# Attention and a mixture of experts in one kernel: v's bias folded into the output's bias, v's copies moved to ACT, and v and q of later pairs computed earlier

## The chip, the cores and the metric

The kernel runs on one core of one Trainium2 chip. The time is device microseconds of one execution, the median over several. A core has five engines with a queue each: PE (matrix multiplies; PEld is its loading of the stationary operand), DVE (vector), ACT (activation functions and copies), POOL (here masks, zeroing and indirect DMAs) and SP (here it only issues DMAs). Each engine's instructions appear in the profile in the order of its queue, and one that waits holds up what is behind it.

## The reference

```python
# x: 8 x 512 x 256 (8 batch rows of 512 tokens), 16 heads of 16, window +-64, 8 experts, top 2
xn = _layernorm(x)
qkv = xn @ Wqkv + bqkv;  q, k, v = jnp.split(qkv, 3, axis=-1)
scores = jnp.einsum('bhid,bhjd->bhij', heads(q), heads(k)) * DH ** -0.5
attn = softmax(where(|i - j| <= 64, scores, min))
attn_out = einsum('bhij,bhjd->bhid', attn, heads(v)) -> b n d,  @ Wout + bout
logits = xn @ router_w + router_b;  top 2 of 8, gates = softmax over the two
h = relu(xn @ w1[e] + b1[e]);  y = h @ w2[e] + b2[e]     # w1: 256 x 1024, w2: 1024 x 256
out = x + attn_out + sum over the two experts of gate * y
```

All data are float32. Each token goes to two experts, so 8192 pairs of a token and an expert have to be computed.

## The kernel before

**Stages.** Until about 44 us the kernel normalizes: for each half u of a batch row b (u = 0 to 15) DVE computes statistics (`stats`, `variances`, `inverse`), ACT the root (`root`, a Sqrt) and the normalized rows (`norm`, line 356), PE turns them (`xt`, line 93), and DVE or ACT takes the turned rows out of PSUM (`keep`, lines 378 and 380). PE computes the router's logits for a row (`lg`), ACT copies them (`keep_logits`, line 401, tile `early`), PE turns them (`lt`), DVE adds the bias (`add_bias`, line 410) and picks the two experts (`choose`, lines 449 to 462, in generator steps called by `pick`, for rows 0 to 3, then 4 and 5, then 6 and 7). The loop over u at lines 1096 to 1134 writes out the order of all this.

Then comes the routing (`route`, line 481; about 44 to 65 us). A scan over all chosen pairs (line 485) and three matmuls (`ranks`) give each pair its slot; slots are sorted by expert into 71 tiles of 128. To turn "slot of each token" into "token of each slot" (`inv`), eight chunks of eight columns each build one-hot tiles: DVE makes `pl` (every second chunk) and two planes of `tl` (lines 550 and 556), ACT the third (line 555, an Identity with a scale), and PE adds eight matmuls per chunk into the PSUM tile `inv`. In chunk 1 `experts` finds each tile's expert and issues the loads of the first two tiles' weights on SP (`load_1`, `load_2`; w1 and w2 of 1 MB each). Steps of `share_out` between chunks compute the gates; its last step turns them (`gps`) and writes them to DRAM (`gd`). From `inv`, DVE works out each slot's token (`tok`, lines 573 to 583), and POOL gathers the first three tiles' normalized rows (`xs`, line 685) and gates (`g`).

From then on two streams are interleaved. One is the experts: for each of 69 tiles PE turns the gathered rows (`turn`: `px`, copied by DVE to `xT`), computes the first layer in two halves (`first_layer`: `h`, ACT's Relu to `hT`), and the second (`second_layer`: `y`; DVE scales it to `yo`, and POOL adds it into the output by an indirect DMA). The other is attention, in 16 pairs p (half of the heads of a batch row b = p // 2): `dense(p, 0)` and `dense(p, 1)` compute q and k; `vals(b, t)` computes v of 128 tokens (into `vA`, two buffers, by b % 2); `maxima(p, n)` (through `search`) multiplies q by k (`sc`) and DVE reduces each row (line 903, tiles `jk` and `nm`); `put_maxima` turns the maxima (`nt`) and adds them into q; `weigh` computes the scores the other way (`st`), ACT the exp, POOL cuts the window's edges (lines 957 and 962); `values` multiplies by v (`av`); `put_sums` to `scale` divide by the row sums through DRAM; `project` multiplies by Wout and DVE adds `bo` (line 1065).

**What sets the order.** The order on ACT, DVE, POOL and SP is the program's own (`manual_schedule`), and `pe` chains PE's instructions in program order as well. The streams are interleaved by the loop at line 1183: 69 rounds of two half-rounds each. A half-round does `weigh`, `search`, `values` and the work of `others(p, r)` (dense, vals, project, each with a cost), one step of `divide`, and then as many pieces of the experts' stream (`expert_pieces`, with costs of 9, 16 and 8) as keep the running cost `sofar` in step with `share`. `LAST` pieces are kept for the end. PSUM tiles of tag "m" have three buffers, shared by nearly all matmuls outside the attention's core.

**What the change touches.** `load_others` (line 143) loads `bv`, 128 copies of v's bias; `vals` adds it by DVE (line 873). `qk_bias` (line 266) turns `braw`, the biases of q and k as 4 rows, into `bqk`. `choices` (line 257; nine instructions on DVE) is called at u = 8, and its tile `choice` is read only by `scale_at_once` at the very end. `turn_b1` (line 279; a turn on PE, a copy on ACT and a DMA `b1d` on SP) is called within `route`. Line 1111 says which `keep` goes to ACT. Lines 1142 to 1147 are the order between the front and the loop:

```python
    dense(0, 1)
    route()
    start_experts()
    search(0)
    for t in range(NT):
        vals(0, t)
```

ACT's table of functions is loaded before the first copy (line 169) and again before the first Sqrt (line 329), and before the gates' Exp (line 472).

Of the kernel before, what the change touches and what calls it, by code (L numbers as in the profile page):

```python
# [22 lines left out]
def kernel(  # L23
# [15 lines left out]
    nc = tc.nc  # L39
# [49 lines left out]
    def matmul(*args, **kwargs):  # L89
        return pe(nc.tensor.matmul(*args, **kwargs))  # L90

    def transpose(*args):
        return pe(nc.tensor.transpose(*args))  # L93
# [24 lines left out]
        xt[b] = pair[:, b % 2]  # L118
        nc.sync.dma_start(out=xt[b], in_=x[b].rearrange("(t p) d -> p t d", p=P))

    braw = const.tile([4, A, 32], F32, tag="braw", name="braw")
    for s in range(2):
        nc.scalar.dma_start(
            out=braw[2 * s : 2 * s + 2],
            in_=bqkv[s * D : (s + 1) * D].rearrange("(a i r) -> i a r", i=2, r=32),
        )
# [7 lines left out]
    raw = p_pool.tile([P, KC, 2 * D], F32, tag="p", name="raw")  # L134
    nc.scalar.dma_start(out=raw, in_=wqkv[:, 0 : 2 * D].rearrange("(k p) m -> p k m", p=P))
    wv = const.tile([P, KC, D], F32, tag="wv", name="wv")
    bv = const.tile([P, D], F32, tag="bv", name="bv")
    b1raw = const.tile([E * HC, P], F32, tag="b1raw", name="b1raw")

    wo = const.tile([P, 2, D], F32, tag="wo", name="wo")  # L140
# [2 lines left out]
    def load_others():  # L143
        nc.sync.dma_start(out=b1raw, in_=b1.rearrange("e (c p) -> (e c) p", p=P))
        nc.sync.dma_start(
            out=wv, in_=wqkv[:, 2 * D : 3 * D].rearrange("(k p) m -> p k m", p=P)
        )
        nc.sync.dma_start(out=bv, in_=bqkv[2 * D : 3 * D].partition_broadcast(P))
        for a in range(A):
            nc.sync.dma_start(  # L150
                out=wo[32 * a : 32 * a + 32],
                in_=wout[64 * a : 64 * a + 64].rearrange("(i r) m -> r i m", r=32),
            )
        nc.sync.dma_start(out=bo, in_=bout.partition_broadcast(P))
# [11 lines left out]
    col_i = const.tile([P, P], I32, tag="col_i", name="col_i")  # L166
    nc.gpsimd.iota(col_i, pattern=[[1, P]], base=0, channel_multiplier=0)
    cols = const.tile([P, P, 16], BF16, tag="cols", name="cols")
    nc.scalar.copy(cols, col_i.unsqueeze(2).to_broadcast([P, P, 16]))

    num_i = const.tile([P, 2], I32, tag="num_i", name="num_i")
# [66 lines left out]
    at = const.tile([P, 2], F32, tag="at", name="at")  # L238
    qat = const.tile([P, 2], F32, tag="qat", name="qat")
    hot = const.tile([P, 2], F32, tag="hot", name="hot")  # L240
    bqk = const.tile([P, 2, 2], F32, tag="bqk", name="bqk")

    kb_ = const.tile([P, 2, 2], F32, tag="kb", name="kb")
    qb_ = const.tile([P, 2, 2], F32, tag="qb", name="qb")
# [20 lines left out]

    def qk_bias():
        bps = ps_m.tile([P, 512], F32, tag="m", name="bps")
        transpose(bps[:, 0:4], braw.rearrange("q a r -> q (a r)"), ident[:4, :4])
        nc.scalar.copy(bqk.rearrange("p s i -> p (s i)"), bps[:, 0:4])
        full = [P, 2, 2]  # L270
        for to, s, by in ((kb_, 1, at), (qb_, 0, qat)):
            nc.vector.tensor_mul(
                to, bqk[:, s].unsqueeze(2).to_broadcast(full), by.unsqueeze(1).to_broadcast(full)
            )
        nc.vector.tensor_add(kb_, kb_, hot.unsqueeze(1).to_broadcast(full))

    b1T = const.tile([P, E * HC], F32, tag="b1T", name="b1T")

# [202 lines left out]
    def route():  # L481
# [15 lines left out]
        next(gating)  # L497
        for s in range(2):
            dense(1, s, by_act=True)
        turn_b1()  # L500

        size_i = wk1.tile([P, E], I32, tag="size_i", name="size_i")
        size = wk1.tile([P, E], F32, tag="size", name="size")
# [32 lines left out]
        for c in range(NA * TOPK // C):  # L536
            h = c % 2
            if h == 0:

                pl = o_pool.tile([P, P, C2], BF16, tag="o", name=f"pl_{c}")  # L540
                nc.vector.tensor_tensor(
                    pl, part[:, ts(c // 2, C2)].unsqueeze(1).to_broadcast([P, P, C2]), cols,
                    ALU.is_equal,
                )

            tl = io.tile([P, 8 * D], BF16, tag="xn", name=f"tl_{c}")
            tl = tl[:, 0 : 3 * C * 2 * W].rearrange("p (s n t) -> p s n t", s=3, n=C)
            full = [P, C, W, 2]
            pairs = tl.rearrange("p s n (w i) -> p s n w i", i=2)
            nc.vector.tensor_tensor(  # L550
                pairs[:, 0], twice[:, ts(c, C)].unsqueeze(2).to_broadcast(full),
                colb.rearrange("p (w i) -> p w i", i=2).unsqueeze(1).to_broadcast(full),
                ALU.is_equal,
            )
            nc.scalar.activation(tl[:, 2], tl[:, 0], AF.Identity, scale=num[:, 0:1])
            nc.vector.tensor_mul(
                pairs[:, 1], pairs[:, 0], hn[:, ts(c, C)].unsqueeze(2).to_broadcast(full)
            )
            for n in range(C):
                matmul(  # L560
                    inv.rearrange("p (s t) -> p s t", s=2), pl[:, :, h * C + n],
                    tl[:, 1:3, n, 0:TILES], start=(c + n == 0),
                    stop=(c * C + n == NA * TOPK - 1),
                )
            if c == 1:
                experts(end)
            if c >= 1:
                next(gating, None)
        of_tile, of_part = inv[:, 0:TILES], inv[:, TILES : 2 * TILES]
        row = wk1.tile([P, TILES], F32, tag="row", name="row")  # L570
        row_i = wk1.tile([P, 2, TILES], I32, tag="row_i", name="row_i")
# [14 lines left out]
    def experts(end):  # L586

        past = p_pool.tile([P, TILES, E], F32, tag="p", name="past")
        starts = wk1.tile([P, TILES], F32, tag="starts", name="starts")
        nc.vector.tensor_scalar(starts, col[:, 0:TILES], float(TS), None, ALU.mult)  # L590
        nc.vector.tensor_tensor(
            past, starts.unsqueeze(2).to_broadcast([P, TILES, E]),
            end.unsqueeze(1).to_broadcast([P, TILES, E]), ALU.is_ge,
        )
        ends = wk1.tile([P, TILES], F32, tag="ends", name="ends")
        ef = wk1.tile([P, TILES], F32, tag="ef", name="ef")
        nc.vector.tensor_reduce(ends, past, AX.X, ALU.add)
        nc.vector.tensor_scalar(ef, ends, float(E - 1), None, ALU.min)
        nc.vector.tensor_copy(eid, ef)
        late["ends"] = ends  # L600
        nc.vector.tensor_copy(filled, end[:, E - 1 : E])
        for i in range(2):
            load_1(i)
            load_2(i)

    def put_gates():
        gps = ps_m.tile([P, 512], F32, tag="m", name="gps")
# [254 lines left out]
    def vals(b: int, t: int):  # L862
        pm = ps_m.tile([P, 512], F32, tag="m", name=f"v_{b}_{t}")
        for k in range(KC):
            matmul(
                pm[:, 0:D], xnT[b][:, k, ts(t, P)], wv[:, k, :],
                start=(k == 0), stop=(k == KC - 1),
            )

        to = vA[b % 2][:, t].rearrange("p h j c -> p h (j c)").rearrange(  # L870
            "p h (u d) -> p h u d", d=DH
        )[:, :, 0:4:3, :]
        nc.vector.tensor_add(
            to,
            pm[:, 0:D].rearrange("p (h j d) -> p h j d", j=2, d=DH),
            bv.rearrange("p (h j d) -> p h j d", j=2, d=DH),
        )

    first = [(h, j, ah) for h in range(2) for j in range(2) for ah in range(2)]
    second = [(j, h, ah) for j in range(2) for h in range(2) for ah in range(2)]  # L880
# [215 lines left out]
    for u in range(UNITS + 3):  # L1096
        b = u // 2
        if u < UNITS:
            norm(u, by_dve=False)
        if u in ROOTS:  # L1100
            root(ROOTS[u])
        if u in INVERSES:
            inverse(*INVERSES[u])
        for n in STATS.get(u, ()):
            stats(n)
            if u in VARIANCES and n in (1, VARIANCES[u][1] - 1):
                variances(*VARIANCES[u])
        if u >= 3 and u % 2 == 1 and b - 1 < B:
            keep_logits(b - 1)
        if 0 < u <= UNITS:  # L1110
            keep(u - 1, by_act=u < 7 or u == UNITS)
        if u >= 5 and u % 2 == 1 and b - 2 < B:
            add_bias(b - 2)
        if u == 3:
            load_others()
        if u == 7:
            places()
        if u == 8:
            qk_bias()
            columns()  # L1120
            choices()
            clear()
        if u >= 8 and u % 2 == 0:
            start_result(u // 2 - 4)
        if u >= 2 and u % 2 == 0 and b <= B:
            logits(b - 1)
        if u >= 4 and u % 2 == 0 and b - 2 < B:
            turn_logits(b - 2)
        if u == 11:
            picking.append(choose(0, 4))  # L1130
        if u == 15:
            picking.append(choose(4, 6))
        if u >= 11:
            pick(3)
# [5 lines left out]
    for b in (6, 7):  # L1140
        start_result(b)
    dense(0, 1)
    route()
    start_experts()
    search(0)
    for t in range(NT):
        vals(0, t)

    pieces = expert_pieces()
    ROUNDS = 4 * (PAIRS + 1) + 1

    divide = {1: gather_sums, 2: invert, 3: put_inverses, 4: spread_inverses, 6: scale}
# [3 lines left out]
    def others(p: int, r: int):  # L1159

        out_ = [[], []]
        if p == -1 and r == 0:
            out_[0].append((0, free_rows))
            out_[1].append((2, destinations))
        if 0 <= p < PAIRS - 2 and r < 2:
            out_[r % 2].append((8, lambda: dense(p + 2, r)))

        if 0 <= p < PAIRS - 2 and r in (1, 2):
            out_[r % 2].append((4, lambda: vals(p // 2 + 1, 2 * (p % 2) + r - 1)))

        if 1 < p < PAIRS and p % 2 == 1:
# [89 lines left out]
```

## Time and profile before

| | |
|---|---|
| timed runs | 918.02, 919.34, 919.76 us; median 919.34 |
| profiled execution | 921.26 us |
| its span | 919.6 us |
| busy: PE, DVE, ACT, POOL | 879.8, 405.4, 377.4, 459.0 us |
| mean granted clock of PE | 0.981 |
| HBM read, written | 172.84 MB, 22.18 MB |
| first `xt` on PE | 9.62 us |
| scan of the routing on DVE | 44.04 us |
| first read of the finished `inv` (`row`) | 64.87 us |
| first `xs` gather issued | 66.14 us |
| `vals(0, 0..3)` on PE | 66.56 to 72.9 us |
| first `h` on PE | 77.48 us |
| last `y` on PE begins | 904.84 us |

How to read the lines: in the windows, each engine has its busy time in the stretch and, in brackets, its count of instructions; then the granted clock of PE (1.00 is full speed), the share of the DMA engines' time that packets took, and GB/s. A timeline line is start, duration, engine, line of the kernel, operation, output <- input, shapes, count, and in square brackets how long the engine was idle before it and what ended that. Most PE work is recorded under line 90 or 93, since two helpers issue it; it is told apart by its tiles. A float32 matmul shows as two records.

### The profile page before, as it was taken

To read this page: it belongs to the slowest core of one execution; us is meant where nothing else is said; L and a number is where in the kernel's file an instruction comes from. 1 tells how busy PE (TensorE), PEld (TensorE's weight loads), DVE (VectorE), ACT (ScalarE), POOL (GpSimd) and SP (SyncE) were. 2 spreads that over 40 slices of the span, in tenths; PEclk is the share of its full clock that TensorE was granted. 3 is DMA by queue.
4 is the path that set the end of the run, shared out by engine and by line. 5 is a ranking of instruction groups with operands and counts; after the bars stand their busy time and mean duration, and the time that the engine had idled before them with its cause. 6 is when DMAs were issued, how large, how long until landed. Compare 5 with 4: busy or idle time off the path is not lost. (4 is left out here: it accounts for less than half of the span.)

```text
span 919.6 us, 20413 instructions
## 1 busy us (share of the span) xinstructions
PE 879.8 (96%) x7260; PEld 707.4 (77%) x7260; DVE 405.4 (44%) x1558; ACT 377.4 (41%) x884; POOL 459.0 (50%) x770
## 2 busy tenths in 40 slices
PE   4778999999999999999999999999999999999995
PEld 2457887878878888877878887878787878888884
DVE  6885343444344434453435343534444344330250
ACT  7541234444444344434444443444434343444421
POOL 4013445456465556455546564466456554656512
PEclk9868999999999999999999999999999999999998
DMA  8953876676666767686858676587667775887794
GB/s 287 321 175 99 263 233 208 218 209 222 209 220 206 202 190 236 206 217 181 249 172 231 193 241 193 169 249 226 203 161 230 223 225 174 237 283 229 230 254 69
DMA packets 154044, 196.38 MB, mean 214 GB/s; under 512 B 26174, under 2 KB 131774, under 8 KB 153942
## 3 DMA queue, kind: packets, MB, share of 16 engines
q1 hardware_dynamic: 133554, 172.20, 57.3%
q0 software_dynamic: 19680, 22.33, 13.0%
q8 instruction: 58, 0.95, 0.4%
q10 hardware_dynamic: 708, 0.54, 0.2%
q14 instruction: 44, 0.36, 0.1%
HBM read 172.84 MB, written 22.18 MB: 212 GB/s over the span
## 5 line engine op out<-in xcount | busy, mean ns | idle before, releaser
L752 ACT ACTIVATE hT<-h,b 128x128 f32<-128x128 f32 x552 | 157.3, 368 | 307.7 <-PE h L90 266.9
L90 PEld LDWEIGHTS h<-xT,w 128*128 128x128 f32 x2208 | 261.2, 193 | 26.0 <-issue 16.8
L90 PE MATMUL h<-xT,w 128*128 128x128 f32 x2208 | 270.2, 278 | 3.4 <-DVE xT L736 3.3
L90 PE MATMUL y<-w,hT 128*128 128x256 f32 x1104 | 252.6, 382 | 0.0
L90 PEld LDWEIGHTS y<-w,hT 128*128 128x128 f32 x1104 | 206.4, 190 | 36.4 <-issue 7.9
L768 POOL DMA_INDIRECT out_dram<-yo,dest x69 | 113.1, 1639 | 224.6 <-DVE yo L767 159.1
L903 DVE CUSTOM_DVE_ANT_0 jk<-sc,mask 128x256 bf16<-128x256 f32 (+1 forms) x512 | 169.7, 387 | 99.2 <-PE sc L90 98.3
L957 POOL TENSOR_SCALAR_AFFINE_SELECT p<-p 128x256 f32<-128x256 f32 (+1 forms) x256 | 138.2, 569 | 119.4 <-ACT p L947 109.3
L947 ACT ACTIVATE p<-st 128x896 f32<-128x896 f32 x128 | 117.4, 917 | 184.7 <-PE sc L90 174.9
L962 POOL TENSOR_SCALAR_AFFINE_SELECT p<-p 128x256 f32<-128x256 f32 (+1 forms) x256 | 140.9, 579 | 0.0
L90 PE MATMUL sc<-k,q 32*128 32x192 f32 (+1 forms) x1024 | 132.2, 376 | 0.0
L90 PE MATMUL st<-q,k 32*128 32x192 f32 (+1 forms) x1024 | 131.4, 374 | 0.0
L767 DVE SCALAR_TENSOR_TENSOR yo<-y,g,b2g 128x256 f32<-128x256 f32 x69 | 33.4, 484 | 183.5 <-PE y L90 93.9
L90 PEld LDWEIGHTS st<-q,k 32*128 32x128 f32 x1024 | 83.8, 184 | 26.3 <-issue 20.6
L90 PEld LDWEIGHTS sc<-k,q 32*128 32x128 f32 x1024 | 84.3, 185 | 2.1 <-issue 1.7
L736 DVE COPY xT<-px 128x256 f32<-128x256 f32 x69 | 29.2, 423 | 121.3 <-PE px L93 121.3
L685 POOL DMA_INDIRECT xs<-xd,tok x69 | 70.0, 1015 | 23.9 <-DVE taken L580 9.0
L695 POOL DMA_INDIRECT g<-gd,gate x69 | 65.8, 953 | 22.8 <-issue 20.7
L90 PE MATMUL av<-p,vA 128*32 128x256 f32 (+1 forms) x1024 | 64.7, 359 | 0.4 <-POOL p L962 0.4
L90 PE MATMUL qk<-xnT,wqk 128*128 128x512 f32 x128 | 63.9, 625 | 0.0
L90 PEld LDWEIGHTS av<-p,vA 128*32 128x32 f32 x1024 | 29.9, 109 | 24.2 <-issue 15.5
L903 DVE DVE_READ_ACCUMULATOR2_ANT nm<- 128x1 f32 x512 | 42.5, 83 | 0.0
(176 smaller groups left out, 592.7 us busy)
## 6 DMA issues: line engine op xcount, KB each, us to landing
w<-in_L_ffn_w_dram SPq DMA_DIRECT2D x138, 1024.0 KB
b<-in_L_ffn_b_dram SPq DMA_DIRECT2D x69, 128.0 KB
x<-in_L_attn_x_dram SPq DMA_DIRECT2D x8, 512.0 KB
xd<-xn SPq DMA_DIRECT2D x8, 512.0 KB
out_dram<-x SPq DMA_DIRECT2D x8, 512.0 KB
out_dram<-sum POOLq DMA_DIRECT2D x8, 512.0 KB, 6.1
bc<-d SPq DMA_DIRECT2D x120, 32.0 KB
b<-b1d SPq DMA_DIRECT2D x69, 4.0 KB
```

Of the source, the lines that this page charges most:

```text
L90: return pe(nc.tensor.matmul(*args, **kwargs))
L685: nc.gpsimd.indirect_dma_start(out=tx, out_offset=None, in_=xd, in_offset=bass.IndirectOffsetOnAxis(ap=tok[:, i : i + 1], axis=0),)
L695: nc.gpsimd.indirect_dma_start(out=tg, out_offset=None, in_=gd, in_offset=bass.IndirectOffsetOnAxis(ap=gate[:, i : i + 1], axis=0),)
L736: nc.vector.tensor_copy(s["xT"], px)
L752: nc.scalar.activation(s["hT"][:, c, :], ph[:, n, :], AF.Relu, bias=s["tb"][:, c : c + 1])
L767: nc.vector.scalar_tensor_tensor(yo, py[:, 0:D], s["tg"], b2g, ALU.mult, ALU.add)
L768: nc.gpsimd.indirect_dma_start(out=by_token, out_offset=bass.IndirectOffsetOnAxis(ap=dest[:, i : i + 1], axis=0), in_=yo, in_offset=None, ...
L903: nc.vector.tensor_tensor_reduce(out=junk[:, 0 : hi - lo], in0=sc[c][:, i, 0 : hi - lo], in1=mask[:, off : off + hi - lo], scale=-1.0, sca ...
L947: nc.scalar.activation(w.rearrange("k c i q -> k c (i q)")[:, :, cut], st.rearrange("k c i q -> k c (i q)")[:, :, cut], AF.Exp,)
L957: nc.gpsimd.affine_select(out=one, in_=one, pattern=[[0, 2], [1, P - off]], compare_op=ALU.is_ge, fill=0.0, base=off, channel_multiplier=-1,)
L962: nc.gpsimd.affine_select(out=two, in_=two, pattern=[[0, 2], [-1, end - P]], compare_op=ALU.is_ge, fill=0.0, base=0, channel_multiplier=1,)
```

## The change

- `braw` gets v's bias as a third pair of rows (a third small DMA on ACT's queue), `bqk` a third entry, and the DMA of `bv` goes. `vals` copies v by ACT, without a bias. Since the weights of a softmax sum to 1, v's bias adds bias @ Wout to every token; the new `out_bias` computes that (two broadcast copies on DVE, two matmuls, an add into `bo`).
- Three more `keep` calls (u = 9, 11, 13) go to ACT; `turn_b1` moves to u = 9; `choices` moves from u = 8 into the loop.
- `vals(0, 0)` and `vals(0, 1)` move ahead of `route`, `vals(0, 2)` and `vals(0, 3)` to where `turn_b1` stood in it. `vals(1, 0..3)`, before in the first two pairs of the loop, come after chunks 1, 3, 5 and 6 of `route`. `dense(2, 0)`, before in pair 0, comes after the first `search`.
- The weight loads of the second tile are issued after chunk 4 in place of within `experts`.
- The first tile's `turn` is done before the loop begins, and so ahead of the second unit of maxima.
- A Sqrt of a constant is issued ahead of ACT's first copy; the second table load, ahead of the first root, falls away.

```diff
-    braw = const.tile([4, A, 32], F32, tag="braw", name="braw")
-    for s in range(2):
+    braw = const.tile([6, A, 32], F32, tag="braw", name="braw")
+    for s in range(3):
         nc.scalar.dma_start(
             out=braw[2 * s : 2 * s + 2],
...
-        nc.sync.dma_start(out=bv, in_=bqkv[2 * D : 3 * D].partition_broadcast(P))
...
+    one = const.tile([1, 1], F32, tag="one", name="one")
+    nc.vector.memset(one, 1.0)
+    nc.scalar.activation(one, one, AF.Sqrt)
     nc.scalar.copy(cols, col_i.unsqueeze(2).to_broadcast([P, P, 16]))
...
-        transpose(bps[:, 0:4], braw.rearrange("q a r -> q (a r)"), ident[:4, :4])
-        nc.scalar.copy(bqk.rearrange("p s i -> p (s i)"), bps[:, 0:4])
+        transpose(bps[:, 0:6], braw.rearrange("q a r -> q (a r)"), ident[:6, :6])
+        nc.scalar.copy(bqk.rearrange("p s i -> p (s i)"), bps[:, 0:6])
...
+    def out_bias():
+
+        wide_b = wk.tile([P, 2, P], F32, tag="junk", name="bv")
+        pm = ps_m.tile([P, 512], F32, tag="m", name="bo_")
+        for i in range(2):
+            nc.vector.tensor_copy(wide_b[:, i, :], bqk[:, 2, i : i + 1].to_broadcast([P, P]))
+        for i in range(2):
+            matmul(pm[:, 0:D], wide_b[:, i, :], wo[:, i, :], start=(i == 0), stop=(i == 1))
+        nc.vector.tensor_add(bo, bo, pm[:, 0:D])
...
         for s in range(2):
             dense(1, s, by_act=True)
-        turn_b1()
+        for t in (2, 3):
+            vals(0, t)
...
             if c >= 1:
                 next(gating, None)
+            if c == 4:
+                load_1(1)
+                load_2(1)
+            if c in (1, 3, 5, 6):
+                vals(1, (1, 3, 5, 6).index(c))
...
-        for i in range(2):
-            load_1(i)
-            load_2(i)
+        load_1(0)
+        load_2(0)
...
-        nc.vector.tensor_add(
-            to,
-            pm[:, 0:D].rearrange("p (h j d) -> p h j d", j=2, d=DH),
-            bv.rearrange("p (h j d) -> p h j d", j=2, d=DH),
-        )
+        nc.scalar.copy(to, pm[:, 0:D].rearrange("p (h j d) -> p h j d", j=2, d=DH))
...
-            keep(u - 1, by_act=u < 7 or u == UNITS)
+            keep(u - 1, by_act=u < 7 or u in (9, 11, 13, UNITS))
...
             qk_bias()
             columns()
-            choices()
             clear()
+        if u == 9:
+            turn_b1()
...
     dense(0, 1)
+    for t in (0, 1):
+        vals(0, t)
     route()
     start_experts()
     search(0)
-    for t in range(NT):
-        vals(0, t)
+    dense(2, 0, by_act=True)
...
     pieces = expert_pieces()
+    pieces.pop(0)[1]()
...
+        if p == -1 and r == 1:
+            out_[0].append((4, out_bias))
+        if p == -1 and r == 2:
+            out_[0].append((0, choices))
...
-        if 0 <= p < PAIRS - 2 and r < 2:
+        if 0 <= p < PAIRS - 2 and r < 2 and (p, r) != (0, 0):
             out_[r % 2].append((8, lambda: dense(p + 2, r)))
 
-        if 0 <= p < PAIRS - 2 and r in (1, 2):
+        if 2 <= p < PAIRS - 2 and r in (1, 2):
             out_[r % 2].append((4, lambda: vals(p // 2 + 1, 2 * (p % 2) + r - 1)))
```

More of the change, by code (lines that the diff above doesn't have):

```diff
@@ L136 @@
     wv = const.tile([P, KC, D], F32, tag="wv", name="wv")
-    bv = const.tile([P, D], F32, tag="bv", name="bv")
     b1raw = const.tile([E * HC, P], F32, tag="b1raw", name="b1raw")
@@ L240 @@
     hot = const.tile([P, 2], F32, tag="hot", name="hot")
-    bqk = const.tile([P, 2, 2], F32, tag="bqk", name="bqk")
+    bqk = const.tile([P, 3, 2], F32, tag="bqk", name="bqk")
     kb_ = const.tile([P, 2, 2], F32, tag="kb", name="kb")
```

## The prediction

> **What bounds the kernel now.** I read the page first (busy shares, the 40 slices, the granted clock), then a table by windows, then the timelines of the engines up to 90 us, and the timeline of PE in the middle.
>
> ```profile
> PE 879.8 (96%) x7260; PEld 707.4 (77%) x7260; DVE 405.4 (44%) x1558; ACT 377.4 (41%) x884; POOL 459.0 (50%) x770
> ...
> PE   4778999999999999999999999999999999999995
> ...
> PEclk9868999999999999999999999999999999999998
> ```
>
> PE is full from slice 5 on, and only the first four slices (92 us) have holes. There the clock is also low, and DVE is the busy engine (9.66 us of the ten from 50 to 60). So there are two stages with different prices: the front, where a chain over DVE, ACT and PE decides, and the rest, where each us of PE work is a us of time. The windows say it in numbers (columns: busy us of PE, PEld, DVE, ACT, POOL, then granted clock, DMA share, GB/s):
>
> ```profile
> 51.40:54.80 3.40, 1.34 (x16) 1.27 (x16) 3.23 (x10) 3.37 (x6) 0.00 (x0) 1.00 0.14 10
> 54.80:58.20 3.40, 1.35 (x11) 1.36 (x12) 3.33 (x7) 1.61 (x3) 1.17 (x2) 0.50 0.43 106
> ...
> 71.90:75.30 3.40, 2.30 (x15) 1.35 (x13) 2.28 (x12) 0.00 (x0) 2.72 (x3) 1.00 0.02 2
> 75.30:78.70 3.40, 1.22 (x10) 1.22 (x11) 2.02 (x6) 0.00 (x0) 2.00 (x3) 1.00 0.15 41
> ```
>
> ```profile
> 80.00:905.00 825.00, 824.53 (x6910) 670.95 (x6910) 346.17 (x1363) 335.94 (x804) 435.85 (x717) 1.00 0.71 214
> ```
>
> From 80 to 905 us PE idles 0.5 us of 825 at full clock. The front on PE's timeline:
>
> ```profile
> 52.70 1.34 PE L90 MATMUL inv<-tl,pl 128*128 128x142 bf16 x16 [2.11 <-ACT tl L555]
> 56.85 2.18 PE L90 MATMUL inv<-tl,pl 128*128 128x142 bf16 x16 [2.81 <-ACT tl L555]
> ...
> 60.27 2.05 PE L90 MATMUL inv<-tl,pl 128*128 128x142 bf16 x16 [1.02 <-ACT tl L555]
> 62.78 2.05 PE L90 MATMUL inv<-tl,pl 128*128 128x142 bf16 x16 [0.47 <-DVE tl L550]
> 64.76 1.86 PE L90 MATMUL sc<-k,q 32*128 32x192 f32 x8
> 66.56 6.32 PE L90 MATMUL v<-wv,xnT 128*128 128x256 f32 x16
> ...
> 73.77 0.44 PE L93 MATMUL px<-ident,xs 128*128 128x128 f32 x2
> 77.48 2.71 PE L90 MATMUL h<-xT,w 128*128 128x128 f32 x16 [3.28 <-DVE xT L736]
> ```
>
> Routing ends with the last inv (DVE's row starts at 64.87); xs is fetched at 66.14 and lands 5.9 us later, at about 72.0; v of row 0 fills that time at half clock; and the first h waits 3.28 us because the copy xT stands on DVE behind the second maxima and free_pl:
>
> ```profile
> 26.36 1.48 DVE L261 COPY choice<-hot 32x32 f32<-32x32 f32 x8
> 27.87 0.69 DVE L380 COPY xnT<-xt 128x512 f32<-128x512 f32 x1
> ...
> 75.87 1.22 DVE L634 TENSOR_TENSOR free_pl<-free_at,cols 128x2048 bf16<-128x2048 bf16 x1
> 77.01 0.42 DVE L736 COPY xT<-px 128x256 f32<-128x256 f32 x1
> ```
>
> In the middle, start to start, a dense half (qk) is worth 1.82 us of PE and one vals tile 0.86 us:
>
> ```profile
> 421.65 1.98 PE L90 MATMUL qk<-xnT,wqk 128*128 128x512 f32 x4
> 423.47 1.03 PE L90 MATMUL v<-wv,xnT 128*128 128x256 f32 x4
> 424.33 0.94 PE L90 MATMUL h<-xT,w 128*128 128x128 f32 x7
> ```
>
> **1. Work taken out of the PE-bound stage.** Four vals of row 1 (4 x 0.86) and one dense half of pair 2 (1.82) leave it: -5.26 us. out_bias comes in: four matmuls of 256 columns, 0.86 us. It is called right after the fourth maxima, and its two DVE copies stand behind that unit's four reductions. In the trace this unit's sc ends on PE at about 91.66 and DVE's last read of nm is at 93.01 + 0.08; two broadcast copies of 128x128 follow (col, a cast of that size, takes 0.22), so about 93.45. PE's order is written out by hand, so it stands still for 1.8 us. Bounds: 0.86 (no stall) to 3.5 (stall, and the copies as slow as xT's 0.42 each); I take 2.66, the row's own times. Stage: -2.6 us. choices (1.75 us of DVE: memset 0.27, copies 1.48) lands before an xT copy; DVE idles 2.66 us before those at 95.76 and 105.52, so it costs nothing; without that cover, 1.75. The 24 other vals turn from a DVE add (0.425 each) into an ACT copy. No row has 128x256 from PSUM by ACT; 128x128 takes 0.26 and 128x512 0.58, so 0.37, at most the 0.60 of the norm. That is 9 us on an engine busy 336 of 825, ahead of an exp whose st matmul stands later on PE anyway: nothing.
>
> **2. Front until the scan (44.04 us).** DVE loses choices (1.75) and three keeps (0.6 each, start to start): 3.55 us, in a stretch where it idles under 0.4 us at a time. ACT gets three copies of 0.48 and b1's 0.2; PE gets b1's turn (0.27; b1raw was issued at 16.8, and the DMA share falls to 0.76 at 20 to 22, so it should be there). Bounds: 0 (ACT and PE only pass the wait on) to -3.55. Followed through the queues: keep(9) can start when xt ends at 26.5 and not at 28.70, lg(4) at 28.25 for 28.61, but then ACT's norms (1.04 us for each unit) set the pace; add_bias(5) comes at 35.6 for 37.13, and the 26 small selection steps behind it are serial on DVE. I take -1.4: the scan at 42.6. The early Sqrt removes one table load (1.28) before root(0), less 0.6 for the new activation and DMA issue; but DVE waits for x at 10.86 for 0.59 us already and would wait longer: 0, at best -0.7. The third braw issue moves raw 0.4 us later, and with it POOL's copy into wqk (11.18), which PE first reads at 38.68: 0. SP loses the bv load; b1d moves between two 512 KB writes, which are over long before 55 us: 0.
>
> **3. Routing, 44 to 65 us.** Here the change adds waits. On ACT the four vA copies of row 1 stand in the queue between the tl steps (after chunks 1, 3, 5 and 6), and each waits for a vals that PE does after the inv of the chunk before. So from chunk 4 on ACT and PE take turns: vals, copy, tl, inv. What a turn costs depends on the clock. PE's inv of a chunk takes 0.67 at full clock and 1.02 at half; vals 0.86 and, from 6.32 / 4, 1.58; tl 0.73 on ACT; vA 0.3 to 0.37. Behind the copies stand only tl, gT and the exp; who waits is PE, then row on DVE.
> At half clock, from the shifted DVE times: inv of chunks 2 and 3 55.35 to 57.4, gps 57.8, vals 59.4, vA 59.75, tl 4 60.45, inv 4 and 5 62.5, vals 64.1, vA and tl 6 65.15, inv 66.2, vals 67.8, vA and tl 7 68.85, inv 69.9: row starts at about 69.9, +5.1 against 64.87. At full clock the same turns (inv 0.67, vals 0.86) end at 66.5: +1.6.
> SP issues the second tile's weights behind gd, once chunk 4's step is reached: about 58 to 60, before 58.62 to 60.80; they are first read by the second tile's h, after 80: 0, and gd lands sooner.
> Which clock? The rows show a stretch 39% busy (51.4 to 54.8), one 53% busy (27.5 to 30.9) and one 36% busy (75.3 to 78.7), each followed by 0.50; those 68% and 76% busy (71.9 to 75.3, 48.0 to 51.4) kept 1.00. Once lost, it came back after stretches that were busy throughout (68.5 to 71.9 and 78.7 to 82.1), and not after 70% or 86% (58.2 to 65.0). In the changed kernel 51.4 to 54.8 holds inv of chunk 1 and most of a vals, about 1.8 of 3.4: 53%. I take half clock, by the row at 53%.
> The Trainium skill ("TensorE: Matmul & The Clock Gate", section "HAM oscillation — how this bites in real kernels") puts the rule as no PE idle gaps over about 3.4 us. The longest gap here would be some 2 us, so by the rule the clock stays full and the whole sum would be -8.3; this trace, which lost the clock after 53% busy, speaks against relying on it.
>
> **4. From routing to the first h.** Before: 64.87 to 77.48, 12.6 us. After, at half clock: sc 1.8 us to 71.7; dense of pair 2 (3.64 at half clock, 1.82 at full; PE is full of f32 work, so between) to about 74.5. xs is issued at row + 1.27 = 71.2; the weights are loaded by then (before, they kept the DMA at 1.04 until 71.4, issued from 55.5; now from 54.1), so it lands like the later ones in 2.7 us: 73.9. px 74.5 to 74.8, xT at once (DVE has nothing ahead of it), sc of the second maxima 1.0 to 1.4, h at about 76.2: -1.3. Then the clock: before, h and px from 77.48 to 83.10 took 5.62 us at 0.50 where two halves and a px take 3.96 at full clock. PE is now busy from 68 on, so that returns: -1.7. Front in all: -3.0 (it holds part 2).
>
> **Sum.** -3.0 - 2.6 = -5.6 us against the profiled execution's 921.26 (span 919.6 and 1.7 around it): 915.7. That execution lies 1.9 above the median of 919.34 of the timed ones; there it gives **913.7 us**.
>
> **Rivals.**
> Full clock through routing. For it: vals in every gap. Row at 66.5, h at 73.5 (xs at 70.4, dense at half clock to 72), clock regained: -4.0 - 1.7 - 2.6 = -8.3: 911.0. Chance 0.27.
> The freed PE time is not gained: the tiles then wait for weights, or dense and vals were cover for something. Against: 214 GB/s in the stage, while 20 to 60 us show up to 390. Then only the front's -3.0 stays, or, with the routing turns 2 us longer, only -0.6 or so is left beside the stage's gain: 916 to 918.5. Chance 0.17.
> Slower: ACT's queue. If every vA copy holds tl longer than worked out (PE, at half clock, still in the chunk before; the copy nearer to 0.60; tl late by a buffer), the turns add to row's start one for one. It decides from row at 69.9 + 5.6 = 75.5, and is measurable from 77.3, 1.9 us a turn over the four turns: 922 or so. For it: three of the four inv groups wait for tl already. Against: tl, vA and inv are short. Chance 0.08. The forecast has 0.48.
>
> **How the numbers follow.** 0.2% (1.8 us) is about what a measurement of this kernel can tell from no change. Range: at the low end full clock with 1 us more of part 2's -3.55 (910.0); at the high end half clock with only 1 us of the sum left (918.3). Faster: 0.48 + 0.27 and two thirds of 0.17, 0.86; same 0.06; slower 0.08.
>
> **What would show it.** The scan at 42 to 43; inv in more than four groups with vals between, row at 66 to 71; granted clock 0.50 or not at 55 to 65; xT straight after px, first h at 73 to 77 with h pairs of 4 us; after that PE without holes but for one of about 1.8 us before bo_; vA on ACT at 0.3 to 0.4. Wrong it would be if row came after 75, if xs landed later than 3 us after issue, or if holes appeared in PE after 90 us.

## The result, and the profile after

The changed kernel takes 922.65 us (median of 19 runs, 918.24 to 929.46) beside 919.12 us of the kernel before (19 runs, 917.31 to 920.09): a ratio of 1.0044, 95% interval 1.0031 to 1.0057 (taken over all runs and not from the two medians; further down, every kernel is compared with runs of the kernel before from its own session). It is slower by 0.4%, where 913.7 us were forecast. The profiled execution has a span of 922.0 us (before 919.6).

The page of the changed kernel, parts 1 and 2, has PE's busy time all but unchanged; the new thing is that one of the late slices, the 36th (807 to 830 us), is no longer full:

```profile
PE 879.1 (95%) x7264; PEld 706.2 (77%) x7264; DVE 390.4 (42%) x1525; ACT 390.4 (42%) x921; POOL 458.8 (50%) x770
...
PE   4868999999999999999999999999999999989996
```

The waits of PE in the changed kernel (engine, line, waited for: us in total, times, longest) name these two as the largest that the kernel before does not have:

```profile
PE h L90 <- DMA w<-in_L_ffn_w_dram: 5.8, 2, 3.5
PE bo__1087 L90 <- issue: 2.4, 1, 2.4
```

On PE's timeline of the changed kernel these are (with the `sc` before and after `bo_`, used further down):

```profile
72.84 0.41 PE L93 MATMUL px<-ident,xs 128*128 128x128 f32 x2 [1.53 <-DMA xs<-xd,tok]
...
74.21 3.57 PE L90 MATMUL h<-xT,w 128*128 128x128 f32 x16
...
88.14 1.03 PE L90 MATMUL sc<-k,q 32*128 32x192 f32 x8
91.57 2.05 PE L90 MATMUL bo__1087<-wo,bv 128*128 128x256 f32 x4 [2.41 <-issue]
93.41 2.47 PE L90 MATMUL h<-xT,w 128*128 128x128 f32 x16
...
102.64 1.03 PE L90 MATMUL sc<-k,q 32*128 32x256 f32 x8
...
816.25 2.05 PE L90 MATMUL h<-xT,w 128*128 128x128 f32 x16
821.77 3.53 PE L90 MATMUL h<-xT,w 128*128 128x128 f32 x16 [3.47 <-DMA w<-in_L_ffn_w_dram]
...
889.77 3.65 PE L90 MATMUL h<-xT,w 128*128 128x128 f32 x16 [2.29 <-DMA w<-in_L_ffn_w_dram]
```

The front gained, by 3.3 us in this execution: the first `h` starts at 74.21 (before 77.48). Then PE stands still ahead of `bo_`, and twice, near 820 and 890, for weights; after each of the last two a group of `h` that takes 2.05 us at full clock takes 3.5 to 3.7.

Where in the program the time went can be read by comparing the start of the same work in both traces (`nt` on PE and `yo` on DVE agree in these places; minus is ahead of the kernel before):

| up to | changed against before, us | what lies between |
|---|---|---|
| first `h` | -3.27 | front and routing |
| 110 to 120 us | +2.17 | `out_bias`: 4.7 of these 5.4 us |
| 750 to 790 us | -3.86 | the loop with four `vals` and a dense half less: -6.0 (0.95 of it the new order alone, as e3 below has it) |
| 825 to 861 us | +0.53 | the wait near 820: +4.4 |
| start of the last `y` on PE | +4.35 | the wait near 890: +3.8 |
| end of the span | +2.4 | what follows the last `y` is 1.9 shorter |

Why should weights be late near 820, when the changed kernel loads the same bytes? SP's own queue shows it. The changed kernel (start, duration, line, what is issued):

```profile
797.12 0.38 SPq L725 DMA_DIRECT2D w<-in_L_ffn_w_dram  x1
...
798.17 0.38 SPq L1032 DMA_DIRECT2D d<-rs  x1
806.85 3.80 SPq L1041 DMA_DIRECT2D bc<-d  x8
810.89 0.41 SPq L737 DMA_DIRECT2D w<-in_L_ffn_w_dram  x1
...
812.92 0.38 SPq L725 DMA_DIRECT2D w<-in_L_ffn_w_dram  x1
```

and the kernel before:

```profile
800.72 0.43 SPq L1020 DMA_DIRECT2D d<-rs  x1
802.85 0.38 SPq L709 DMA_DIRECT2D w<-in_L_ffn_w_dram  x1
...
806.82 4.27 SPq L1029 DMA_DIRECT2D bc<-d  x8
811.33 0.41 SPq L721 DMA_DIRECT2D w<-in_L_ffn_w_dram  x1
```

`d<-rs` writes the inverse sums to DRAM, the eight `bc` copies read them back, and SP waits in between until the write has landed. In the kernel before a load of w1 stood between the two. In the changed kernel nothing does: 8.7 us pass from `d<-rs` to the first `bc`. The next load of w2, whose buffer came free when a `y` ended at about 805.8, is issued at 810.89: the first 1.0 us of that delay SP still waits for the landing, the other 4.0 it spends on issuing `bc`, which the wait has pushed behind the end of the `y`. Over the whole run (waits of SP's queue) SP waits for `d<-rs` 26.7 us in the kernel before and 53.0 in the changed one:

```profile
SPq L1041 <- DMA d<-rs: 53.0, 9, 8.9
```

Such a wait is not a loss in itself: in both kernels 4.7 to 10.5 us pass between the two in every one of the fifteen pairs, and PE of the kernel before waits for no weights at all. It costs where a load stands behind it that PE needs soon.

So the program's order on SP is another than before, though the diff moves none of these DMAs. The reason is the loop's bookkeeping: a half-round does its own work and then as many pieces of the experts' stream as keep `sofar` in step with `share`. The change takes a dense half (8), four `vals` (4 each) and a turn (1) out of the costs and puts in `out_bias` (4): 21 units less, and every later piece slides against the steps of `divide`.

### The profile page after: what moved, and what is told of

Read it like the earlier page. It is cut to its first block, busy times and chain, and to the rows that moved or that the text cites. A ratio compares the mean times of both kernels' runs of the same rounds, so it can differ in the third digit from the quotient of the medians.

```text
span 922.0 us, 20417 instructions
## 1 busy us (share of the span) xinstructions
PE 879.1 (95%) x7264; PEld 706.2 (77%) x7264; DVE 390.4 (42%) x1525; ACT 390.4 (42%) x921; POOL 458.8 (50%) x770
## 5 line engine op out<-in xcount | busy, mean ns | idle before, releaser
L90 PEld LDWEIGHTS h<-xT,w 128*128 128x128 f32 x2208 | 264.7, 195 | 27.8 <-issue 20.4
L90 PE MATMUL h<-xT,w 128*128 128x128 f32 x2208 | 273.8, 280 | 5.8 <-DMA w<-in_L_ffn_w_dram 5.8
L969 POOL TENSOR_SCALAR_AFFINE_SELECT p<-p 128x256 f32<-128x256 f32 (+1 forms) x256 | 133.0, 543 | 118.3 <-ACT p L959 116.7
L974 POOL TENSOR_SCALAR_AFFINE_SELECT p<-p 128x256 f32<-128x256 f32 (+1 forms) x256 | 138.0, 562 | 0.0
```

What stands on the lines that cost most here:

```text
L969: nc.gpsimd.affine_select(out=one, in_=one, pattern=[[0, 2], [1, P - off]], compare_op=ALU.is_ge, fill=0.0, base=off, channel_multiplier=-1,)
L974: nc.gpsimd.affine_select(out=two, in_=two, pattern=[[0, 2], [-1, end - P]], compare_op=ALU.is_ge, fill=0.0, base=0, channel_multiplier=1,)
```

## The experiments

Two causes were set against each other. **'Phase'**: the slide of the loop's order makes the weights late; without it the forecast gain is there. **'Lead'**: PE, with less to do, runs ahead, and the weights cannot follow, in whatever order. Beside them stands `out_bias` at its place.

**e1_align**: the changed kernel, with the costs of before in the loop (no-ops in place of what moved), so that SP's order is that of the kernel before.

```diff
-        if 0 <= p < PAIRS - 2 and r < 2 and (p, r) != (0, 0):
-            out_[r % 2].append((8, lambda: dense(p + 2, r)))
+        if 0 <= p < PAIRS - 2 and r < 2:
+            out_[r % 2].append((8, (lambda: dense(p + 2, r)) if (p, r) != (0, 0) else lambda: None))
...                                  # vals of row 1 likewise: (4, lambda: None)
-            out_[0].append((4, out_bias))
+            out_[0].append((0, out_bias))
...
-    sofar = 0
+    sofar = 1
```

> The changed kernel, with the bookkeeping of the loop's costs as before: work that was moved out of the loop keeps its old cost as an empty entry, out_bias costs 0, so that experts' pieces, weight loads and division steps stand against the rounds exactly as in the kernel before (SP's order in the loop is the same). In the changed kernel PE waits 5.8 us for weights at 818 to 822 and 887 to 890 and then runs at a clock of 0.66 to 0.68 for some 5 us; up to 819 it was 3.9 to 4.4 us ahead. Theory 'phase' (the shifted costs put weight loads behind the bc DMAs on SP at the wrong moment): these waits go, 913.5 to 916.5. Theory 'lead' (weights cannot follow a PE that is 4 us ahead, in whatever order): still 919 to 924, with PE waiting for w after 800.

**e2_bias**: the changed kernel with `out_bias` called ahead of the loop, right after `dense(2, 0)`; its cost of 4 stays in the loop as a no-op.

```diff
     dense(2, 0, by_act=True)
+    out_bias()
...
-            out_[0].append((4, out_bias))
+            out_[0].append((4, lambda: None))
```

> The changed kernel with out_bias called right after dense(2, 0), where PE waits 1.5 us for xs anyway, and an empty entry of cost 4 in its old place. Theory 'stall': the 2.4 us in which PE waits for DVE before bo_ and the half clock behind it (together 3.5 us, from 1.3 ahead to 2.2 behind between 91 and 101 us) go; yo at 100 us is 1 to 1.5 ahead of the kernel before. Whether the time shows it: by 'phase' 918 to 920 (3.5 less than 922.65, the late weights stay), by 'lead' no change, 921 to 924, since PE only arrives earlier at the same late weights.

**e3_before_shift**: the kernel before, with the costs of the changed kernel for the same work.

```diff
-            out_[r % 2].append((8, lambda: dense(p + 2, r)))
+            out_[r % 2].append((8 if (p, r) != (0, 0) else 0, lambda: dense(p + 2, r)))
...                                  # vals of row 1 and the first turn likewise 0
+        if p == -1 and r == 1:
+            out_[0].append((4, lambda: None))
```

> The kernel before, with nothing changed but the costs in the loop's bookkeeping: dense(2, 0), the four vals of row 1 and the first turn count 0, and an empty entry of 4 stands where out_bias is in the changed kernel, so that SP's order in the loop is that of the changed kernel. Theory 'phase': PE waits for weights after 800 us here too, 922 to 928 for 919.1. Theory 'lead': no PE wait of over 1 us, 918 to 920.5.

**e4_both**: e1 and e2 together.

> e1 and e2 together: costs as before, and out_bias behind dense(2, 0). Theory 'phase': 910 to 913, that is 3 to 4 less than e1. Theory 'lead': 919 to 923, no better than e1.

| kernel | median us (range) | ratio to before | 95% interval |
|---|---|---|---|
| changed | 922.65 (918.24 to 929.46) | 1.0044 | 1.0031 to 1.0057 |
| e1_align | 919.15 (915.24 to 921.31) | 1.0013 | 0.9998 to 1.0027 |
| e2_bias | 918.69 (914.44 to 923.52) | 1.0011 | 0.9992 to 1.0030 |
| e3_before_shift | 922.72 (921.44 to 923.86) | 1.0050 | 1.0032 to 1.0068 |
| e4_both | 912.86 (911.63 to 914.86) | 0.9949 | 0.9930 to 0.9968 |

e2 (918.69) and e3 (922.72) came out where 'phase' had put them. e3 computes exactly what the kernel before computes, with the same instructions; only the order of the loop is slid, and it is 0.5% slower, with the same wait in the same place (PE's timeline of e3):

```profile
822.87 3.65 PE L90 MATMUL h<-xT,w 128*128 128x128 f32 x16 [3.65 <-DMA w<-in_L_ffn_w_dram]
```

By itself e3 does not rule 'lead' out: in its profile PE is 3.4 us ahead of the kernel before at that place (`yo`, 815.45 for 818.88), 1.9 of it from the first `h` on, though the front is the same. e4 does, below. e1 by itself came out where 'lead' had put it, above the range of 'phase': the wait near 820 shrank from 3.47 to 0.83 us, but only 0.3% came back, since the stall at `bo_` cost this kernel still more than the changed one (from the `sc` before `bo_` to the next but one, PE goes from 3.1 us ahead of the kernel before to 3.1 behind). With `bo_` out of the way as well, e4 gains 0.6% over e1 and stands at 0.9949, within the range that had been forecast for the change. On the timeline of e4, `bo_` comes while PE would wait for `xs` anyway, and its own wait is short; and near 820, with the order of before, PE waits 0.40 us for weights although it is 9.8 us ahead of the kernel before there. So it is not the lead:

```profile
69.18 1.10 PE L90 MATMUL bo__905<-wo,bv 128*128 128x256 f32 x4 [0.49 <-PE qk L90]
...
813.27 2.02 PE L90 MATMUL h<-xT,w 128*128 128x128 f32 x16 [0.40 <-DMA w<-in_L_ffn_w_dram]
```

**f1_vals_back**: e4 with `vals(1, 0..3)` back in the loop (in place of e4's no-ops), so that routing has no turns of ACT and PE.

```diff
-            if c in (1, 3, 5, 6):
-                vals(1, (1, 3, 5, 6).index(c))
```

> e4 (costs as before, out_bias behind dense(2, 0)) with the four vals of row 1 back in the loop, where they were before, so that ACT has no vA copy between the tl steps. The loop then holds 4 x 0.86 = 3.4 us more PE work. In e4 the last inv starts at 65.15. Theory 'turns cost more than they free' (as forecast at half clock: 5 us of routing): row comes 4 to 5 earlier, about 61 to 62, and the time is 1 to 2 less than e4's 912.9. Theory 'turns are cheap' (routing at full clock, as the 1.00 of e4's windows says): row comes 2 to 2.5 earlier and the time is 1 to 2 more, 914 to 915.

It took 912.63 us, 0.9938 (0.9918 to 0.9958), which cannot be told from e4; neither theory's time came. The two traces show a trade: the last `inv` pair starts at 60.61 in f1 where e4's last `inv` starts at 65.15, but f1 then runs `qk` at half clock (3.75 us for 1.98), and its first `h` comes only 1.05 us sooner, at 70.47 for 71.52. From 91 us on f1 leads by 4.25 us (1.9 of it are gaps of e4 at 79 to 82 us within an `h` group, beside a weight load, for which the profile gives no releaser); the four `vals` in the loop then take 2.9 us of that lead, 0.73 each, close to the 0.86 a tile of the forecast. So `vals` in the routing neither gained nor lost measurably.

**f2_spread_late, f3_before_shift_spread, f4_both_spread**: a first attempt on what holds SP. In the changed kernel, in e3 and in e4, `bc` and the scaling behind it come one half-round later, for every pair.

```diff
-    divide = {1: gather_sums, 2: invert, 3: put_inverses, 4: spread_inverses, 6: scale}
+    divide = {1: gather_sums, 2: invert, 3: put_inverses, 5: spread_inverses, 7: scale}
```

> The changed kernel with the spread of the inverses (the eight bc DMAs) one half-round later, at 5 for 4, and scale at 7 for 6. In the changed kernel SP stands at the first bc from 798.5 to 806.9, waiting for d<-rs to land, and the w2 load behind it goes out at 810.89, 5 us after its buffer came free; h then waits 3.5 us for w at 818 to 822. Theory 'SP blocked by bc': bc no longer waits, the w2 loads go out when y ends, that wait and the lost clock behind it go: 5 less, 916 to 919. Theory 'DMA bandwidth' (the loads would land no sooner): 921 to 924, with PE waiting for w near 820 as before.

> e3 (the kernel before with the costs of the changed one) and the spread one half-round later, as in f2. e3 took 922.7 against 917.8 and PE waited 3.6 us for w at 819 to 823, behind a bc that waited 8.7 us on SP. 'SP blocked by bc': back to 917 to 919. 'DMA bandwidth': 921 to 924.

> e4 with the spread one half-round later. e4 has next to no waits of PE for w (0.4 us). 'SP blocked by bc': no change, 912 to 914, or up to 1 less. If the later spread puts DVE's scale or the projections behind their data, slower: 915 or more.

All three were slower than the kernels that they were made from: 926.84 us, 1.0087 (1.0069 to 1.0105); 929.61 us, 1.0123 (1.0105 to 1.0142); 919.47 us, 1.0010 (0.9998 to 1.0022). Neither theory had expected that; only the expectation of f4 had named a late scaling as a way to be slower. The wait near 820 did go in f2 and f3, but other waits came. Near 400 us POOL shows one; first e4, then f4:

```profile
393.27 1.40 POOL L1079 DMA_DIRECT2D out_dram<-sum  x1
400.49 1.65 POOL L784 DMA_INDIRECT out_dram<-yo,dest  x1 [5.83 <-issue]
```

```profile
395.07 1.42 POOL L1079 DMA_DIRECT2D out_dram<-sum  x1
406.85 1.66 POOL L784 DMA_INDIRECT out_dram<-yo,dest  x1 [10.36 <-issue]
```

The write of `yo` follows the write of `sum` to the same output by 11.8 us in f4 and by 7.2 in e4, and behind it on POOL stand the cuts of the window's edges, which PE's `av` needs: f4 falls 2.0 us further behind e4 just there. PE's waits in f2 name the same and a second:

```profile
PE av L90 <- POOL p L974: 3.3, 5, 2.5
PE po L90 <- DVE yo L783: 1.8, 1, 1.8
```

So these runs did not decide it: with fifteen pairs moved, a second cost covered what was to be measured. The next three move one pair alone.

**g1_before_shift_one, g2_after_one, g3_bias_one**: e3, the changed kernel and e2, with `bc` and the scaling of one pair, the one whose `bc` stands at 807 us, one half-round later.

```diff
+    late_divide = {1: gather_sums, 2: invert, 3: put_inverses, 5: spread_inverses, 7: scale}
...
-            step = divide.get(2 * r + part)
+            step = (late_divide if p == 14 else divide).get(2 * r + part)
```

> The kernel before with the changed kernel's costs in the loop (e3: ratio 1.005, PE waits 3.65 us for w near 822), and in addition the bc copies and the scale of one pair alone, the fourteenth (the one whose bc stood on SP from 799.1 to 807.8 us waiting for d<-rs), one half-round later. 'SP is held there': the w2 load behind them is issued some 5 us sooner, the wait near 822 falls under 1 us, the ratio comes back to 0.9985 to 1.002. 'The order as a whole' (the loss is spread over the loop, or the DMA engines are simply full there): the wait stays or moves, ratio 1.003 to 1.007.

> The changed kernel with the same one pair's bc and scale one half-round later, nothing else. 'SP is held there': the 3.47 us wait near 822 and the half clock behind it go, the 2.29 us near 890 and the stall at bo_ stay: ratio 0.9995 to 1.002 against 1.0044. 'The order as a whole': 1.003 to 1.006.

> The changed kernel with out_bias ahead of the loop (e2: ratio 1.0011) and the same one pair later. If the two stalls, at bo_ and near 820, are all that stood between the changed kernel and the predicted time, this comes to 0.995 to 0.998, as e4 did with another order of the whole loop (0.9949). 'The order as a whole': 1.000 to 1.003.

| kernel | median us (range) | ratio to before | 95% interval | without the edit |
|---|---|---|---|---|
| g1 | 918.19 (915.93 to 921.55) | 0.9995 | 0.9977 to 1.0014 | e3: 1.0050 |
| g2 | 913.52 (910.56 to 916.62) | 0.9949 | 0.9930 to 0.9968 | changed: 1.0044 |
| g3 | 909.58 (908.61 to 913.75) | 0.9908 | 0.9883 to 0.9934 | e2: 1.0011 |

SP's queue in g2: two weight loads now stand between `d<-rs` and `bc`, and go out as soon as their buffers are free.

```profile
797.50 0.38 SPq L1032 DMA_DIRECT2D d<-rs  x1
...
805.37 0.38 SPq L737 DMA_DIRECT2D w<-in_L_ffn_w_dram  x1
...
807.53 0.38 SPq L725 DMA_DIRECT2D w<-in_L_ffn_w_dram  x1
...
808.59 8.65 SPq L1041 DMA_DIRECT2D bc<-d  x8
817.47 0.41 SPq L737 DMA_DIRECT2D w<-in_L_ffn_w_dram  x1
```

The w2 load is issued at 805.37 in place of 810.89, the w1 load that PE waited for at 807.53 in place of 812.92, and PE does not wait near 820: what it waits for weights over the whole run is 0.5 us, for 5.8.

```profile
PE bo__1087 L90 <- issue: 1.7, 1, 1.7
...
PE h L90 <- DMA w<-in_L_ffn_w_dram: 0.5, 2, 0.2
```

g2 keeps a steady 0.5 to 0.7 us ahead of the changed kernel from 100 to 800 us and is 5.9 ahead at 825: 5.2 us are gained in that place. In g1 it is 5.5 us against e3, and its one wait for weights is 0.97 us at 884. 'SP is held there' is thereby shown, in the kernel before (g1 against e3) as in the changed one. The theory that the DMA engines are simply full there falls: the same bytes go through in the same stretch. g2 even gains more than was expected, 0.95% for 0.2 to 0.5, and g3 came out under its range too: in g2's profile the wait near 890 is 0.23 us, which makes 3.7 us more, and this part is not explained. In the changed kernel that load of w1 took 11.3 us to land (issued at 878.49, first read at 889.77), in g2 9.2 at most (872.98 to 882.18), in the same order of the queue and with nearly the same distances; why it is 2 us quicker, no run here settles. e2 and e3, with the slid order, wait 0.51 us and not at all there; whether the long wait belongs to the changed kernel or to this one execution is open.

g1 and g2 have the same order of the loop and the same late pair, and differ only by the change itself: 0.9949 to 0.9995, intervals that do not meet, -0.46% or -4.2 us. That is what the change is worth in this order of the loop, with `out_bias` as written. g3, with `out_bias` ahead of the loop, is 0.87% under g1 and the best version here: 909.58 us, faster than both kernels.

## Why the prediction was wrong

**Work taken out of the PE-bound stage: the size held, the sum did not.** The -5.26 us for four `vals` and a dense half are there: -6.0 between 120 and 750 us, -5.1 without the 0.95 that e3 gains there by the order alone; in e1 and e4, with the order of before, it is -4.2 and -4.75. What failed is the step behind it, that the stage gives each us of PE work back as a us of time and that nothing else in it changes. The costs in `others` were read as labels of work. They also place each weight load against the steps of `divide`, and by sliding 21 units the change put `bc` directly behind `d<-rs` on SP at 798 to 807 us, with two loads behind it. The working followed SP's queue through the routing (part 3) and not through the loop, where the moved work has no DMAs but moves others'. Price in the profiled execution: 4.4 us near 820, and 3.8 near 890, of which only the first is shown to be the slide's: e3, which has the slide alone, has the first wait, not the second, and is 0.5% slower. The cause of the second is open. The prediction had named holes in PE after 90 us as a sign that it is wrong, and these are the holes.

The rival "the tiles then wait for weights" named the sign on PE and set it at 916 to 918.5, as a gain that does not come. The argument against it, 214 GB/s in the stage and up to 390 at other times, was a mean over 825 us. The windows of the changed kernel around the wait (columns as before, at the end clock, DMA share and GB/s):

```profile
806.00:808.00 2.00, 2.00 (x23) 1.88 (x25) 0.48 (x1) 0.17 (x1) 0.88 (x1) 1.00 0.05 16
808.00:812.00 4.00, 4.00 (x40) 3.65 (x37) 1.76 (x9) 3.04 (x10) 2.45 (x6) 1.00 0.52 96
...
816.00:821.00 5.00, 2.30 (x24) 1.86 (x16) 2.76 (x8) 1.57 (x5) 4.62 (x6) 1.00 0.96 313
821.00:826.00 5.00, 4.23 (x23) 4.07 (x25) 0.44 (x2) 0.60 (x3) 0.95 (x1) 0.66 1.10 368
```

While SP stands, the engines still move the two loads issued at 795 and 797 (273 GB/s over 798 to 806); then they have next to nothing to do until the next loads are issued, and from 816 they are full: the loads came late and together. A mean rate says nothing about when a load may start. No rival had a loss in this place. 922 us was given to ACT's queue, with `row` after 75.5; `row` came at 68.48, so that this figure nearly meets the measured 922.65 is chance.

**`out_bias`, mis-sized.** 2.66 was taken (bounds 0.86 to 3.5, though the upper one comes to 3.1 by its own rows): 1.8 of stall and 0.86 of matmuls. The stall was 2.41, since DVE, before the four reductions, was still in the 17 short steps of `destinations`, the copy `xT` and the scaling `yo`, until about 90.0 (DVE's timeline of the changed kernel):

```profile
89.12 0.20 DVE L692 CAST dest<-row 128x71 int32<-128x71 f32 x1
...
89.96 0.35 DVE L915 CUSTOM_DVE_ANT_0 jk<-sc,mask 128x192 bf16<-128x192 f32 x1
...
91.20 0.36 DVE L283 COPY bv<-bqk 128x128 f32<-128x128 f32 x2
```

And the stall cost the clock, which had not been priced. The windows from 88.4 to 95.2 us, first of the changed kernel, then of g2 (busy us of PE, PEld, DVE, ACT, POOL, granted clock, DMA share, GB/s):

```profile
88.40:91.80 3.40, 0.99 (x9) 0.62 (x8) 3.05 (x17) 0.00 (x0) 1.48 (x1) 0.89 0.57 171
91.80:95.20 3.40, 3.40 (x16) 3.04 (x17) 0.42 (x1) 0.00 (x0) 2.10 (x3) 0.60 0.87 252
```

```profile
88.40:91.80 3.40, 2.27 (x15) 1.43 (x13) 2.86 (x14) 0.00 (x0) 1.22 (x1) 1.00 0.16 39
91.80:95.20 3.40, 2.87 (x22) 2.79 (x22) 0.93 (x5) 0.00 (x0) 2.36 (x3) 1.00 0.90 304
```

A stretch 29% busy lost the clock, one 67% busy kept it here. The whole price is read on PE from the `sc` ahead of `bo_` to the next but one, between which both kernels do the same work except `bo_`. It takes 14.50 us in the changed kernel (88.14 to 102.64, shown above), 15.9 in e1 and 9.76 in the kernel before:

```profile
90.71 1.03 PE L90 MATMUL sc<-k,q 32*128 32x192 f32 x8
...
100.47 1.03 PE L90 MATMUL sc<-k,q 32*128 32x256 f32 x8
```

So `out_bias` costs 4.7 us in the changed kernel and 6.2 in e1, for the 2.66 of the sum (`yo` shows only 3.5, since the `yo` ahead of it is itself late). On the chip, moving `out_bias` is worth 0.33% (e2 against the changed kernel), 0.41% (g3 against g2) and 0.64% (e4 against e1): 3.0 to 5.9 us.

**Front until the scan: right.** Forecast 42.6 (-1.4), measured 42.43 (-1.6):

```profile
42.43 0.69 DVE L496 TENSOR_TENSOR_SCAN upto<-goon,took 128x256 bf16<-128x256 bf16 x1
```

One trace of each proves little here, since with this front the scan came at 41.84 to 45.80 in nine traces, and at 43.47 to 44.04 in four with the front of before; the medians, 42.43 and 43.8, differ by the 1.4 that was forecast. The early Sqrt moved the first `xt` from 9.62 to 8.81, a little more than its best, -0.7, but whether that part reached the scan is not shown apart from the rest.

**Routing: the turns right, the clock not settled.** The turns of vals, copy, `tl` and `inv` are there. In this execution the clock is lost after the stretch 51.4 to 54.8 (41% busy), and `row` starts at 68.48, between the full clock's 66.5 and the half clock's 69.9. The copies take 0.37, as estimated:

```profile
L889 ACT COPY vA<-v 128x256 f32<-128x256 f32 x32 | 11.9, 371 | 10.7 <-PE v L90 10.2
...
51.40:54.80 3.40, 1.38 (x12) 0.92 (x9) 3.26 (x8) 1.98 (x4) 0.31 (x1) 1.00 0.00 0
54.80:58.20 3.40, 2.53 (x20) 2.48 (x21) 3.33 (x8) 1.47 (x3) 0.33 (x1) 0.81 0.94 302
58.20:61.60 3.40, 2.27 (x16) 1.71 (x16) 2.89 (x6) 1.71 (x3) 0.00 (x0) 0.50 1.06 341
```

The longest gap of PE there is 2.50 us. The rule in the Trainium skill ("TensorE: Matmul & The Clock Gate", section "HAM oscillation — how this bites in real kernels") of no idle gaps over some 3.4 us would have kept the full clock, which was lost here. But e4, with the same routing and a longest gap of 2.51, kept it, after a stretch that was less busy still (36%):

```profile
51.40:54.80 3.40, 1.24 (x10) 0.79 (x7) 3.26 (x9) 1.98 (x4) 0.31 (x1) 1.00 0.00 0
54.80:58.20 3.40, 2.36 (x21) 2.18 (x22) 3.33 (x7) 1.61 (x5) 0.33 (x1) 1.00 0.91 321
```

So neither the longest gap nor the busy share of such a stretch tells which it will be. From the scan to `row` the routing takes 23.56 us in e4 and f2, where the clock stayed 1.00, 24.9 in e1, e2, g2 and g3, 26.0 in the changed kernel and f4, and 20.83 to 20.86 in all five traces without `vals` between the chunks. The forecast's two cases were 23.9 at full and 27.3 at half clock: with one and the same routing the rival of a full clock occurs, and the half clock only for a part of the routing.

**Routing to the first `h`: better than forecast in its start, not in its clock.** `px` waits 1.53 us for `xs`, `xT` follows at once, and the first `h` starts at 74.21 for the forecast 76.2. The -1.7 for a clock regained did not come: 71.8 to 75.2 us ran at 0.82 and 75.2 to 78.6 at 0.67, though 86% and 69% of the stretches before were busy; and `h`, `px`, `h` took 5.5 us from 74.21 where before they took 5.6. The two errors cancel: behind these PE is 3.4 us ahead, for the 3.0 that were forecast for the front, and that is luck. `choices` in the loop and the second tile's weights cost nothing, as assumed.

## What to carry to other kernels

Where a loop places one stream's work by the summed cost of another's, taking work out slides everything behind it; look, on each DMA queue, at what then stands behind a transfer that waits for another's landing, before the freed time is counted as gained. The cheapest test is the old kernel with the new costs: it shows what the slide alone does. And a wait that sits in one place is undone in that place: moved for one pair, `bc` gave 0.5 to 1.0%; moved for all pairs, it cost 0.4 to 0.7%.

## What the runs showed of the hardware that was not expected

- A queue that waits for a landing holds up bandwidth, not only itself: with SP standing at 798 to 807 and then issuing `bc`, the DMA engines moved 16 GB/s at 806 to 808 and 96 at 808 to 812, were full from 816, and PE waited 3.47 us for a load of 1 MB that took 8.9 us from issue to first use. The Trainium skill ("DMA: Bandwidth & Descriptors", section "Issuing engines are not separate DMA queues") says that spreading DMAs over the issuing engines saves only the time to initiate them, which is usually small; here what stood on one engine's queue was worth 5.2 and 5.5 us near 820 (g2 against the changed kernel, g1 against e3), some 0.6% of the run. No run here issues these DMAs from another engine.
- SP also stood 4.06 us on a small bias load at 815.08, behind three loads of 1 MB and eight `bc` copies, and the eight `bc` copies took 8.65 us to issue in g2, where two such loads had just gone out, for 3.80 in the changed kernel.
- The wait of 3.47 us near 820 was followed by a granted clock of 0.66 over 821 to 826, with `h` at 3.53 us for 2.05: by the clock the wait cost 1.5 us more. In e2 a wait of 3.66 us at the same place was followed by 0.57 over 816 to 821 and 0.50 over 821 to 826, and the place cost 8.1 us by `yo`, for 4.9 in the changed kernel.
